# Two attention blocks on one core: the divisors of the linear attention computed behind the softmax sums instead of behind the gather

## The chip, the cores and the metric

The kernel runs on one core of one Trainium2 chip. The metric is the device time of one execution in microseconds. Four runs of the kernel before took 2598.89 to 2601.56 us, with a median of 2601.18.

## The reference, cut to what matters

The input x has 8 images of 512 channels and 64 x 64 = 4096 positions, float32. Two attention blocks follow each other.

```python
# first block: softmax attention over max-pooled keys and values
f = conv1x1(x, Wf, bf)                       # 64 channels
g = maxpool2x2(conv1x1(x, Wg, bg))           # 64 channels, 1024 positions
v = maxpool2x2(conv1x1(x, Wh, bh))           # 256 channels, 1024 positions
s = einsum('bcn,bcm->bnm', f, g)
beta = softmax(s, axis=-1)
o = einsum('bcm,bnm->bcn', v, beta)
x = gamma * conv1x1(o, Wv, bv) + x

# second block: linear attention
Q, K, V = wq @ x + bq, wk @ x + bk, wv @ x + bv
delu = lambda t: 10 * relu(t) + exp(10 * minimum(t, 0))
Qf, Kf = delu(Q).T, delu(K)                  # 64 features
KV = einsum('bmn,bcn->bmc', Kf, V)
norm = 1 / einsum('bnd,bd->bn', Qf, Kf.sum(-1) + EPS)
attn = einsum('bnd,bdc,bn->bcn', Qf, KV, norm)
return x + gamma1 * attn
```

Two divisions matter here. The softmax divides by the sum of exponentials of each position. The second block divides by Qf times the sum of Kf, one divisor for each position; these are the divisors that move.

## The kernel before, in words

**Chunks and steps.** Each image is cut into 8 chunks of 512 positions, 64 chunks in all. The function `step(s)` puts the work of one step in order. In step s the first block is finished for chunk s (its attention, projection and store), the scores of chunk s+1 are computed, and the keys and values of chunk s+9 are prepared. The letter j is the place of chunk s in its image, 0 to 7. The second block lags by one image: while image b goes through the first block, the output of image b-1 is computed in pairs of chunks and added to what is stored. So it is at work in steps 8 to 63 (`c_here`), and the pairs of the last image are done after the loop in another way.

**The order.** The kernel's order is written out by hand. `at(t, fn)` notes a piece of work with a due time t inside the step; the pieces are sorted by t and issued in that order on each engine, which runs its own list in order. A due time is therefore only a place in the list, the same for all five queues: PE (TensorE), DVE (VectorE), ACT (ScalarE), POOL (GpSimd) and SP (SyncE, which issues most DMAs).

**The softmax sums.** The exponentials of chunk s+1 (`weigh`, lines 402 to 411; scores on TensorE at L407, exponentials at L411) are added up on VectorE (L445 to L450). `total` multiplies the result by ones on TensorE. For most chunks (`by_quarters`, chunks 2 to 55) it does so in four matmuls of 128 columns, each into 32 output partitions (L464, shape 128x32), so that the reciprocal (L474) runs on 128 x 128 and not on 128 x 512. `spread_inverses` then writes four rows to DRAM (L479, tile rd) and reads them back onto all partitions (L481, tile rb); `keep_inverses` copies them into PSUM on ScalarE (L485, tile rtot); `look` reads both sums and reciprocals on ScalarE for a check of range (L489, L490). `normalize_block` multiplies the exponentials by rtot in four pieces (L499). For the other chunks the sums are one matmul on all 512 columns (L459) and the reciprocal takes 128 x 512 with no DMA.

**Attention and projection.** `attend` computes the seven products M1 to M7 of one level of a Strassen-like scheme (L523), each of eight 128x256 matmul instructions in the trace, with combinations on VectorE (L532 to L556). `project` does the same with seven products N1 to N7 (L586). Three of them are added into the bank of the first, after each of three evictions by ScalarE (L596), each followed by an addition on GpSimd (L599); VectorE adds the others (L602, L607). The differences of the normalized exponentials for the next chunk follow on VectorE (L505 to L514).

**Around the divisors.** `gather` (L727, tile pg, shape 128x64) multiplies transposed features and transposed x. `features` (L633) and what follows (L643 to L652) make Q and K features; qq holds the Q features of a pair of chunks, 64 partitions each. `normalize(pair, at, t, t_invert, t_out)` has three pieces:

- `product` at t: four matmuls into 32 output partitions each (L818, tile pd), by a matrix kb that holds the sums of K features. The trace shows them as eight instructions, since each float32 matmul is two.
- `inversion` at t_invert: the reciprocal on VectorE (L825, tile rq_pd, which shares its one buffer with L474's rq), a DMA that writes eight rows to DRAM (L827), and two DMAs that read them back onto 64 partitions each (L831, tile rn).
- `out` at t_out: VectorE multiplies qq by rn (L837).

`normalize` is called in steps with j=0 for the first pair of the image, and with j = 1, 3, 5 for the next ones: 4 times for each of 7 images, 28 in all. `finish`, in steps with odd j, multiplies qq by KV (L855), copies to y (L858) and adds y to the output in DRAM with two DMAs of GpSimd's queue (L861).

**Due times near the change.** In the steps concerned: gather 12.6; M6 14.4; sums 16.1 in odd j with `c_here`, else 17.85 (19.55 in the last image's even steps); M5 16.2; M7 17.9; M4 19.6; reciprocal of the sums 18.0, their DMAs 18.01; transposes of v (uv, L371) 18.7; VectorE's last combination of the attention products 22.5; `keep_inverses` 23.0; first normalization 24.3. Those are the values for the middle of the run.

**Buffers.** All PSUM tiles come from one pool of 8 banks, scratch tiles from a pool of 7. A tile takes the buffer that came free earliest in the written order, and its first instruction waits for the last reader of the tile before it.

Of the kernel before, what the change touches and what calls it, by code (L numbers as in the profile page):

```python
# [51 lines left out]
def tile_two_attention_blocks(  # L52
# [32 lines left out]
    TOTAL = B * NCHUNK  # L85
# [91 lines left out]
    def half(e):  # L177
        return slice(e * D, (e + 1) * D)

    def run(ctx, general):  # L180
# [14 lines left out]
        def bank(name):  # L195
            return psum.tile([P, CH], F32, tag="m", name=name)

        def scratch(name):
            return temp.tile([P, CH], F32, tag="t", name=name)
# [610 lines left out]
        def normalize(pair, at, t, t_invert, t_out):  # L810

            m = {}

            def product():

                pd = m["pd"] = bank(f"pd_{pair}")[:, 0:P]
                for i in range(NT):
                    nc.tensor.matmul(  # L818
                        pd[bass.ts(i, QP), :], kb[:, D - QP // 2 : D + QP // 2],
                        qq[pair][:, bass.ts(i, P)], start=True, stop=True,  # L820
                    )

            def inversion():
                rd = work1.tile([P, P], F32, tag="rq", name=f"rq_pd_{pair}")
                nc.vector.reciprocal(rd, m["pd"])  # L825
                d = rows.tile([2 * NT, P], F32, tag="rn", name=f"rn_{pair}_row")
                nc.sync.dma_start(out=d, in_=rd[0 : P : QP // 2, :])  # L827
                rn = m["rn"] = scratch(f"rn_{pair}")
                for e in range(2):
                    row = d.rearrange("(i e) n -> e i n", e=2)[e : e + 1]  # L830
                    nc.sync.dma_start(  # L831
                        out=rn[half(e)].rearrange("p (i n) -> p i n", n=P),
                        in_=row.to_broadcast([D, NT, P]),
                    )

            def out():
                nc.vector.tensor_tensor(qq[pair], qq[pair], m["rn"], ALU.mult)  # L837

            at(t, product)
            at(t_invert, inversion)  # L840
            at(t_out, out)
# [114 lines left out]
        def step(s):  # L956
            here, after = 0 <= s < TOTAL, 0 <= s + 1 < TOTAL
            a = s + LEAD
# [3 lines left out]
            pair = (b_c * NCHUNK + j) // 2  # L962
# [57 lines left out]
            if c_here and here and j == 1 and a <= TOTAL:  # L1020
                make_KV(b_c, at, 5.5, 5.55)
            if c_here and here and j == 0:
                normalize(pair, at, 12.65, 13.7, 38.6)
            if c_here and here and j % 2 == 1 and j < NCHUNK - 1:
                normalize(pair + 1, at, 12.65, 13.7, 38.6)
            if c_here and here and j % 2 == 1:

                cover = a == TOTAL
# [119 lines left out]
        for s in range(-LEAD, TOTAL + 1):  # L1148
            step(s)
# [59 lines left out]
```

## Time and profile before

| | |
|---|---|
| median of 4 runs | 2601.18 us (2598.89 to 2601.56) |
| the profiled execution | 2602.07 us |
| its span | 2600.3 us |
| mean granted TensorE clock | 0.995 |
| busy: TensorE, VectorE, ScalarE, GpSimd | 2564.4, 1954.2, 1587.0, 771.8 us |
| L818 (divisors) on TensorE | 224 instructions, median 285 ns |
| L464 (sums in quarters) on TensorE | 432 instructions, median 285 ns |
| L825, L474 (reciprocals, 128x128) | 28 of 951 ns, 54 of 957 ns (medians) |
| L474 (reciprocals, 128x512) | 10 of 3367 ns |
| L837 (multiplication by rn) | 28 of 682 ns |

The span is that of the profiled execution alone; the difference to its time lies before the first and behind the last instruction. In the timeline a row gives start, length, engine, line, operation and tiles, and the number of instructions merged into it; a bracket at its end tells how long the engine had stood idle before it, and what ended that. TensorE's instructions overlap: a row's length reaches beyond the start of the next, so costs on TensorE are read as differences of starts.

### The profile page before, as it was taken

The numbers are of one execution on the slowest core, as the hardware profiler recorded it, in microseconds if no ns is written. First come the engines' busy times: TensorE is split into PE (matmuls) and PEld (weight loads), VectorE is DVE, ScalarE is ACT, GpSimd is POOL, SyncE is SP. The second block draws the span as 40 slices with busy tenths as digits, with TensorE's granted clock in tenths as the row PEclk, the third lists the DMA queues.
The fourth block names the chain that finished last, engine by engine and source line by source line (L and its number), as shares of the span: only waits on it lengthen the run. The fifth ranks groups of instructions, "written<-read, shape, count | busy, mean of one in ns | idle before, by whom it ended". The sixth has DMA issues, their size and how long they took to land.

```text
span 2600.3 us, 32002 instructions
## 1 busy us (share of the span) xinstructions
PE 2564.4 (99%) x11207; PEld 1766.8 (68%) x11207; DVE 1954.2 (75%) x3000; ACT 1587.0 (61%) x2724; POOL 771.8 (30%) x618
## 2 busy tenths in 40 slices
PE   9999999999999999999999999999999999999997
PEld 6667767667667667677666676666676676766664
DVE  5777777777777777777777777777777777788874
ACT  3365566566565676675675665666755656656662
POOL 5422323322323323223233233323233232221112
PEclk9999999999999999999999999999999999999998
DMA  5154455575555675565665565755657655665658
GB/s 179 46 140 98 128 146 144 132 178 140 148 165 133 165 176 127 157 165 130 173 153 152 148 142 152 188 133 150 159 132 183 148 145 146 146 147 144 162 141 270
DMA packets 488730, 390.68 MB, mean 150 GB/s; under 512 B 342072, under 2 KB 357360, under 8 KB 488560
## 3 DMA queue, kind: packets, MB, share of 16 engines
q1 hardware_dynamic: 471312, 329.03, 45.9%
q0 software_dynamic: 15232, 58.72, 12.1%
q8 instruction: 91, 1.49, 0.2%
q10 hardware_dynamic: 2016, 0.79, 0.1%
q14 instruction: 79, 0.65, 0.1%
HBM read 173.41 MB, written 133.39 MB: 118 GB/s over the span
## 4 chain that ended last, share of the span: by engine, by line
PE 91%; DVE 3%; DMA 1%; issue 1%; ACT 0%; POOL 0%; DVEq 0%; ACTq 0%; SPq 0%
PE M L523 30%; PE N L586 14%; PE H L316 13%; PE s L407 9%; PE pk L633 8%; PE fg L272 7%; PE pg L727 5%; PE pa L855 4%; PE tot L464 1%; DVE E L499 1%; PE pkv L791 1%; PE pa L934 1%; PE pd L818 0%; DMA rb<-rd 0%; PE tot L459 0%
## 5 line engine op out<-in xcount | busy, mean ns | idle before, releaser
L599 POOL TENSOR_TENSOR xb<-xb,n 128x512 f32<-128x512 f32 x192 | 245.6, 1279 | 470.4 <-ACT n L596 459.9
L523 PE MATMUL M<-T,S 128*128 128x256 f32 x1536 | 365.6, 389 | 0.0
L499 DVE TENSOR_TENSOR E<-E,rtot 128x1024 f32<-128x1024 f32 x256 | 307.6, 1223 | 71.1 <-ACT rtot L485 69.0
L523 PEld LDWEIGHTS M<-T,S 128*128 128x128 f32 x1536 | 283.6, 191 | 81.4 <-ACT E L411 24.9
L695 ACT COPY xT<-u 128x1024 uint16<-128x1024 uint16 x252 | 328.3, 1354 | 1.4
L682 ACT COPY w<-xb 128x1024 uint16<-128x1024 uint16 x252 | 244.8, 1042 | 87.7 <-DVE xb L602 87.7
L596 ACT ACTIVATE n<-N,gb_v 128x256 f32<-128x256 f32 x384 | 160.8, 470 | 216.7 <-PE N L586 216.7
L411 ACT ACTIVATE E<-s 128x512 f32<-128x512 f32 x512 | 257.0, 624 | 33.5 <-DVE T L514 18.9
L674 POOL COPY kT<-uk 128x512 uint16<-128x512 uint16 x56 | 67.3, 1202 | 620.7 <-DMA uk<-wk 620.7
L586 PE MATMUL N<-to,w_v 128*128 128x256 f32 x1024 | 243.6, 380 | 4.1 <-ACT n L596 3.9
L407 PE MATMUL s<-f,g 64*128 64x512 f32 x1024 | 240.2, 604 | 2.8 <-DVE o L532 2.8
L523 PE MATMUL M<-E,vT 128*128 128x256 f32 x1024 | 231.8, 379 | 2.1 <-DVE E L499 2.1
L633 PE MATMUL pk<-xb,w_kqk 128*128 128x512 f32 x512 | 230.5, 593 | 1.9 <-DVE xb L607 1.9
L305 POOL TENSOR_TENSOR tha<-xa 128x512 f32<-128x512 f32 x59 | 80.2, 1360 | 500.7 <-PE M L523 463.9
L602 DVE TENSOR_TENSOR xb<-xb,N 128x512 f32<-128x512 f32 x256 | 173.9, 683 | 56.7 <-POOL xb L599 54.4
L586 PEld LDWEIGHTS N<-to,w_v 128*128 128x128 f32 x1024 | 193.2, 190 | 34.0 <-ACT n L596 7.0
L523 PEld LDWEIGHTS M<-E,vT 128*128 128x128 f32 x1024 | 194.4, 190 | 29.7 <-issue 3.4
L272 PE MATMUL fg<-xa,w_fg 128*128 128x512 f32 x472 | 212.5, 593 | 0.0
L445 DVE TENSOR_TENSOR r<-E 128x1024 f32<-128x1024 f32 x64 | 78.4, 1225 | 166.3 <-ACT E L411 166.3
L586 PE MATMUL N<-o,w_v 128*128 128x256 f32 x768 | 188.4, 381 | 1.8 <-ACT n L596 0.9
L586 PEld LDWEIGHTS N<-o,w_v 128*128 128x128 f32 x768 | 144.6, 190 | 56.6 <-issue 35.7
L485 ACT COPY rtot<-rb 128x512 f32<-128x512 f32 x54 | 31.8, 589 | 241.3 <-DMA rb<-rd 241.3
(160 smaller groups left out, 4515.3 us busy)
## 6 DMA issues: line engine op xcount, KB each, us to landing
xb<-in_x_dram SPq DMA_DIRECT2D x64, 1024.0 KB
out_dram<-xb SPq DMA_DIRECT2D x63, 1024.0 KB
xa<-in_x_dram SPq DMA_DIRECT2D x59, 1024.0 KB
out_dram<-y POOLq DMA_DIRECT2D x56, 1024.0 KB, 10.5
rb<-rd SPq DMA_DIRECT2D x54, 256.0 KB
w_v<-in_L_conv_wv_dram SPq DMA_DIRECT2D x8, 1024.0 KB
rn<-rn_row SPq DMA_DIRECT2D x56, 128.0 KB
x_early<-in_x_dram SPq DMA_DIRECT2D x4, 1024.0 KB
```

Of the source, the lines that this page charges most:

```text
L272: nc.tensor.matmul(fg, w_fg[:, k, :], x_a[a][:, k, :], start=(k == 0), stop=(k == KT - 1))
L316: nc.tensor.matmul(m[i], w_h7[i][:, k, :], th[a][i][:, k, :], start=(k == 0), stop=(k == hk - 1))
L407: nc.tensor.matmul(sc[e], g[half(e), i, :], fs[s][half(e), :], start=True, stop=True)
L411: nc.scalar.activation(es[s][:, 2 * i + e, :], sc[e], AF.Exp)
L499: nc.vector.tensor_tensor(b, b, r, ALU.mult)
L523: nc.tensor.matmul(m[i], v7[i][:, k, :], te[s][i][:, k, :], start=(k == 0), stop=(k == hm - 1))
L586: nc.tensor.matmul(a[:, k, :], w_v7[i][:, bass.ts(k, P)], b, start=not more and k == 0, stop=True, skip_group_check=more or k > 0,)
L599: nc.gpsimd.tensor_tensor(of_x(*ij), of_x(*ij), u, ALU.add)
L602: nc.vector.tensor_tensor(of_x(*ij), of_x(*ij), m[i], op)
L633: nc.tensor.matmul(pk, w_kqk[:, i, e * D : (e + 2) * D], x_b[s][:, i, :], start=(i == 0), stop=(i == KT - 1),)
L682: nc.scalar.copy(w, x_b[s][:, k, :].bitcast(U16).rearrange("p (n h) -> p h n", h=2))
L695: nc.scalar.copy(v[:, k], u)
```

## The change

The divisors' matmuls, their reciprocal and the DMAs behind it get later due times. The matmuls go from 12.65, directly behind the gather, to 17.87 (19.57 in the first step of the last image); the reciprocal and the three DMAs from 13.7 to 22.6. The multiplication by the result stays at 38.6. No instruction is added or removed.

```diff
             if c_here and here and j == 0:
-                normalize(pair, at, 12.65, 13.7, 38.6)
+                normalize(pair, at, 17.87 if a < TOTAL else 19.57, 22.6, 38.6)
             if c_here and here and j % 2 == 1 and j < NCHUNK - 1:
-                normalize(pair + 1, at, 12.65, 13.7, 38.6)
+                normalize(pair + 1, at, 17.87, 22.6, 38.6)
```

In the order of the built program this means, for the steps before the last image: on TensorE, from gather, **pd**, M6, M5, tot, M7, M4 to gather, M6, M5, tot, **pd**, M7, M4 where j=0; from gather, **pd**, M6, tot, M5, M7, M4 to gather, M6, tot, M5, **pd**, M7, M4 where j is 1, 3 or 5. On VectorE the reciprocal L825 goes from ahead of L537 to behind L556, directly ahead of the first L499. On SP the row write and the two reads go from ahead of L479 to behind L371. In the last image the sums are the 512-column form (L459), and the block goes from behind the gather to behind L459 (first step) or behind M5 (odd steps).

## The prediction

> **What bounds the kernel now.** I read the page, the waits and then the timeline around the divisors. From the page:
>
> ```profile
> span 2600.3 us, 32002 instructions
> ...
> PE 2564.4 (99%) x11207; PEld 1766.8 (68%) x11207; DVE 1954.2 (75%) x3000; ACT 1587.0 (61%) x2724; POOL 771.8 (30%) x618
> ...
> PE 91%; DVE 3%; DMA 1%; issue 1%; ACT 0%; POOL 0%; DVEq 0%; ACTq 0%; SPq 0%
> ```
>
> TensorE holds 91% of the chain. What an edit is worth is thus read in TensorE's own row, as what it adds to it plus the places where it stands still. The view of waits:
>
> ```profile
> DVE rq L474 <- DMA rn_row<-rq_pd: 19.5, 22, 2.2
> ...
> POOL xb L599 <- DMA rn<-rn_row: 10.4, 1, 10.4
> ```
>
> The first line is the wait that the change takes away: both reciprocals write one buffer (tag rq), so the one of the sums (L474) waits until the divisors' row (L827) has been read out of it, 22 times, 19.5 us. Whether that costs anything is a question to TensorE. Its timeline in step 9 (j=1: divisors), step 10 (none), and in step 55, where the attention products run with neither block between them:
>
> ```profile
> 460.65 0.43 PE L818 MATMUL pd<-qq,kb 128*32 128x128 f32 x8
> 461.00 1.99 PE L523 MATMUL M<-T,S 128*128 128x256 f32 x8
> 462.93 0.42 PE L464 MATMUL tot<-r,ones 128*32 128x128 f32 x8
> 463.28 3.72 PE L523 MATMUL M<-T,S 128*128 128x256 f32 x16
> 466.84 1.89 PE L523 MATMUL M<-T,vT 128*128 128x256 f32 x8
> ...
> 498.30 3.72 PE L523 MATMUL M<-T,S 128*128 128x256 f32 x16
> 501.95 0.42 PE L464 MATMUL tot<-r,ones 128*32 128x128 f32 x8
> 502.30 1.99 PE L523 MATMUL M<-T,S 128*128 128x256 f32 x8
> 504.13 1.89 PE L523 MATMUL M<-T,vT 128*128 128x256 f32 x8
> ...
> 2276.44 5.45 PE L523 MATMUL M<-T,S 128*128 128x256 f32 x24
> 2281.73 1.46 PE L523 MATMUL M<-T,vT 128*128 128x256 f32 x6
> ```
>
> Read starts, not durations. Twenty-four products alone take 2281.73 - 2276.44 = 5.29. With the sums among them, 504.13 - 498.30 = 5.83: a 128x32 block alone between 128x128 products costs 0.55 (0.54 by the rounded starts, 0.553 unrounded). The divisors, which now stand between pg (128x64) and the products, add only 461.00 - 460.65 = 0.35: there the shape of the array changes anyway.
>
> Last, where TensorE stands still. From the start of the score matmuls (L407) of one step to the next, every step with j=1, 3 or 5 of images 1 to 6 takes 41.08, every plain even one 37.29: no waiting that varies. The six j=0 steps take 41.17, 40.78, 40.42, 40.80, 40.55 and 42.32. The first:
>
> ```profile
> 419.61 0.95 DVE L825 RECIPROCAL rq_pd<-pd 128x128 f32<-128x128 f32 x1
> ...
> 422.96 1.32 SPq L831 DMA_DIRECT2D rn<-rn_row  x2
> 423.03 0.96 DVE L474 RECIPROCAL rq<-tot 128x128 f32<-128x128 f32 x1 [2.20 <-DMA rn_row<-rq_pd]
> ...
> 426.56 0.35 SPq L481 DMA_DIRECT2D rb<-rd  x1
> ...
> 429.93 0.59 ACT L485 COPY rtot<-rb 128x512 f32<-128x512 f32 x1 [3.74 <-DMA rb<-rd]
> ...
> 431.33 0.92 PE L586 MATMUL N<-to,w_v 128*128 128x256 f32 x3 [0.30 <-ACT n L596]
> ```
>
> The late reciprocal makes the spread sums (rb) late; ScalarE stands at L485; the eviction n (L596) is queued behind it; TensorE's sixth projection product needs that eviction. In step 48 the same place idles 1.45. Step 24 has no such wait, so the excess over 40.42 is what there is to win: 0.75 + 0.36 + 0 + 0.38 + 0.13 + 1.90 = 3.52 us.
>
> **The change part by part.** All 28 divisor blocks (j = 0, 1, 3, 5 of seven images) move.
>
> *TensorE, j=0 of images 1 to 6.* The block follows the sums directly, in the same 128x32 shape. Not in the trace: two such blocks in a row. Within the sums' block the second round of four starts 0.113 after the first, so two rounds cost 0.23; the other bound is today's 0.356, which would be no change. I take 0.226, the nearest row, being of the same form: 6 x -0.13 = -0.8.
>
> *TensorE, j=1, 3, 5.* Here the sums stand at 16.1 and M5 at 16.2, so the block at 17.87 falls between M5 and M7, alone, not behind the sums. It costs 0.553, the sums' own row, in place of 0.356: +0.197, 21 times: +4.1. Bounds: no more than today (0), and twice the difference (+8.3), for want of a row that shows more.
>
> The Trainium skill (TensorEngine Tiling (Array Packing), Key Properties) says that a change of tiling mode drains the engine. It speaks against this half of the change: in odd steps the block adds two changes of mode in place of one, in j=0 none in place of one. The trace agrees that a change costs, 0.13 beside pg (0.356 - 0.226) and 0.16 each for the lone block (half of 0.553 - 0.226). If every change had one price between these, the odd steps would lose 2.7 to 3.4 and the j=0 steps win 0.8 to 1.0, and the sum below would be 0.5 to 1.0 lower.
>
> *VectorE, quarters.* L474 no longer waits for the row, so rtot comes earlier. In step 8: M6 starts 0.35 earlier, the sums' matmul at 419.70, its reciprocal at about 420.2 (0.5 behind, as at 502.44) instead of 423.03. By that step's own delays rd is issued at 421.2, rb at 423.4, and rtot is copied at 426.7 instead of 429.93. The eviction needs its product at 429.4, so 2.7 us are to spare; step 48, where rb took 5.0 to land instead of 3.4, still has about 1. I take the whole stall as gone: -3.5; bounds 0 and -3.5. In odd steps rtot comes 1.1 earlier and TensorE does not notice.
>
> *VectorE, the moved reciprocal (0.95).* It now stands behind L556 and ahead of the first normalization (L499). In step 8 L556 now ends about 425.9, so the reciprocal is done at 426.9, when rtot has just come; the normalization still starts 3.6 before its 430.55. In step 9 L556 ends at 470.53 + 0.20, the reciprocal at 471.68, where L499 began at 471.82: hidden by what was the wait for rtot. It waits for the look (L490) and for rd, both done by then. Without that cover 0.95 would fall on L499; its last one ends at 478.18 and its first user on VectorE (L505) starts at 482.18, so 4 us remain.
>
> *The last image.* Step 56 has no rd/rb. Its 3.37 us reciprocal starts 0.36 earlier with the sums, but from there VectorE is busy without a gap to L532 at 2340.20, for which the score matmuls stand still. The 0.95 that filled a wait before now lies in that row: 0.95 - 0.36 = +0.6 (bounds -0.4, the stall at L553 alone, and +0.95). In steps 57, 59 and 61 the 0.92 wait ahead of L652 takes it up; their +0.2 on TensorE is in the 21 above.
>
> *SyncE and DMAs.* The row write (4 KB) and its two reads (2 x 128 KB) pass behind rd, rb and the transpose uv, which gain. They now start at 471.7 in odd steps, after this:
>
> ```profile
> 469.53 2.54 POOL L861 DMA_DIRECT2D out_dram<-y  x2
> ```
>
> These two accumulations keep the DMA engines busy until about 482. The last image shows the pair under such a load: row write at 2473.13, reads at 2478.99, landed by 2485.37 (the 10.4 line above): 5.9 and 12.2. From 472.3 that gives the reads at 478.2, landing at 484.5. Behind the reads SyncE has the transposes u, first issued at 482.29: 2.2 to spare after 1.9 of issuing. L837 needs the data at 490.2: 5.7 to spare. In step 56 the next load of x moves from 2322.5 to about 2330, and is used at 2360. No cost; if the cover went, see the third rival.
>
> The Trainium skill (DMA: Bandwidth & Descriptors, Queues, rings and completion order) has each engine take the queues in turn, packet by packet. By that the reads would land soon after their issue, about 480 in place of 484.5; the sum is the same.
>
> *PSUM and scratch.* The pools hand out other buffers from the moved tile on. N1 of odd steps now waits for the look (done 465.97, needed 472.0), pk for an addition done at 479.5 (needed 482.15), pg of step 57 for the divisors' reciprocal, 6 us ahead. No cost.
>
> **Sum** against the profiled execution, 2602.07 (span 2600.3 and 1.8 around it; 0.89 above the median 2601.18): -0.8 + 4.1 - 3.5 + 0.6 = +0.4, that is 2602.5 there, and 2601.6 beside the median.
>
> **Rivals.**
> 1. *The stalls of j=0 stay* (rb lands late for another reason, as the 5.0 in step 48 hints): 2601.6 + 3.5 = 2605.1. Against it: 2.7 us to spare.
> 2. *A lone divisor block costs no more than beside pg.* The 4.1 falls away: 2597.5. For it: bounds only; against it: the sums' row, the same form.
> 3. *The reads of the divisors come too late* (the other side, slower). They start 10 us later, into the accumulations. If they land after 490.2, L837 holds L511, L514 and L532 queued behind it on VectorE; L532 frees the bank for the third pair of score matmuls (loaded at 494.62, L532 ends 493.49, so 1.1 to spare). It decides from 19.0 us between row write and landing (490.2 - 472.3 + 1.1), where 12.2 were seen; at 20 it would cost 1.0 in each of 18 odd steps: 2601.6 + 18 = 2620.
> 4. *The freed wait is worth more than the j=0 stalls* (VectorE 19.5 us earlier in sum). If all of it reached TensorE: 2601.6 + 3.5 - 19.5 = 2585.6. Against it: odd steps of one length to 0.01 us.
>
> **How the numbers follow.** A measurement of this kernel tells about 0.2% (5.2 us) from no change. Forecast 0.58, rival 1 0.10, rival 2 0.08, rival 3 0.16, rival 4 0.08. Rivals 1 and 2 stay within 0.2%, so same 0.76, slower 0.16, faster 0.08. The range leaves out rivals 3 and 4, 0.24 together, of which the mild end of 3 still falls inside: from rival 2, 2597.5, to the doubled price of the lone block, 2601.6 + 4.1 = 2605.7, so 2606.
>
> **What would show it.** Rq's line of waits on rn_row gone; step 8 and its like at 40.3 from score to score; odd steps at 41.28 (41.08 would be rival 2); L837 without a wait for rn; step 56's score matmuls idle 0.6 longer. A line of waits of L837 on rn, or odd steps of unequal length, would make the forecast wrong.

## The result, and the profile after

The changed kernel took 2604.15 us (median of 40 runs, 2603.03 to 2606.98), the kernel before 2601.17 (median of 60 runs beside them, 2597.62 to 2604.25). The ratio is 1.0014, with a 95% interval of 1.0009 to 1.0018: slower by 2.3 to 4.7 us, about 3.0, where 0.4 was forecast. That lies within the 0.2% that the prediction counted as no change, and within its range of 2597.5 to 2606, but it is seven times its sum, so a term of that sum was mis-sized.

The profiled execution of the changed kernel took 2603.87 us (before: 2602.07). From its page:

```profile
span 2602.0 us, 32060 instructions
...
PE 2562.2 (98%) x11207; PEld 1764.3 (68%) x11207; DVE 1959.1 (75%) x3000; ACT 1587.3 (61%) x2724; POOL 775.0 (30%) x618
...
PE 87%; DVE 6%; ACT 1%; issue 1%; DMA 0%; POOL 0%; DVEq 0%; ACTq 0%; SPq 0%
```

TensorE still has the chain, but VectorE has doubled its share of it, from 3 to 6%, and is busy 4.9 us longer with the same 3000 instructions. Some VectorE instruction got longer. The view of waits has what the change promised:

```profile
DVE E L499 <- ACT rtot L485: 29.1, 26, 1.3
...
DVE rq L474 <- PE tot L464: 20.1, 25, 0.9
...
PEld N L586 <- ACT n L596: 7.0, 9, 1.3
```

(engine, tile and line, who ended the wait: total us, times, longest). L474's line on the divisors' row is gone; the normalizations' wait for rtot fell from 69.0 us to 29.1, and the wait of the projection's weight loads (PEld) for the eviction from 10.4 to 7.0. The products themselves had waited for it in steps 8 and 48 (0.30 and 1.45 us); in images 1 to 6 they no longer do.

Where the time went is read step by step, as the difference of starts of the first score matmul (L407) of one step and the next, in the timelines of the two profiled executions:

| steps | before | after | forecast |
|---|---|---|---|
| 8, 16, 24 (j=0) | 41.17, 40.78, 40.42 | 40.79, 40.80, 40.79 | 40.3 each |
| 32, 40, 48 (j=0) | 40.80, 40.55, 42.32 | 40.28, 40.80, 40.78 | 40.3 each |
| 18 odd ones (j=1, 3, 5) | 41.08 each | 41.28 each | 41.28 each |
| 18 even ones (j=2, 4, 6) | 37.29 each | 37.29, step 42: 37.73 | 37.29 each |
| 56 and 57 together | 66.37 | 66.98 | +0.6, +0.2 |
| 59, 61 | 32.55, 32.55 | 32.74, 32.74 | +0.2 each |

The odd steps came out to a hundredth. The six j=0 steps did not: 246.04 became 244.25, a gain of 1.8 where 4.3 was forecast. Only step 32 has the forecast length; the five others stop at 40.8. The timeline of the changed kernel in step 8 shows why:

```profile
417.30 1.39 POOL L305 TENSOR_TENSOR tha<-xa 128x512 f32<-128x512 f32 x1 [7.36 <-PE M L523]
417.60 1.64 DVE L450 TENSOR_TENSOR r<-r 128x512 f32<-128x512 f32 x1
...
419.39 0.43 PE L464 MATMUL tot<-r,ones 128*32 128x128 f32 x8 [0.44 <-DVE r L450]
...
419.61 0.43 PE L818 MATMUL pd<-qq,kb 128*32 128x128 f32 x8
...
420.10 0.94 DVE L474 RECIPROCAL rq<-tot 128x128 f32<-128x128 f32 x1
...
426.10 0.59 ACT L485 COPY rtot<-rb 128x512 f32<-128x512 f32 x1 [0.35 <-DMA rb<-rd]
...
428.91 0.84 ACT L596 ACTIVATE n<-N,gb_v 128x256 f32<-128x256 f32 x2 [2.22 <-PE N L586]
...
429.57 2.75 PE L586 MATMUL N<-to,w_v 128*128 128x256 f32 x12
```

and the timeline of the kernel before, at the same place. (Step 8 starts at 409.72 in the changed kernel and at 410.54 before; so 0.82 is to be added to the changed kernel's times to compare.)

```profile
418.40 0.69 DVE L450 TENSOR_TENSOR r<-r 128x512 f32<-128x512 f32 x1
418.47 1.75 POOL L305 TENSOR_TENSOR tha<-xa 128x512 f32<-128x512 f32 x1 [7.74 <-PE M L523]
```

From 420.10 down, the changed kernel does what was forecast: the reciprocal follows the sums, rtot is copied 16.4 us into the step (before: 19.4), the eviction waits for its product and no longer the other way round, and the projection products run without a gap. But the sums' matmul now waits 0.44 for L450, the last addition of the exponentials on VectorE. L450 takes 1.64 us instead of 0.69. Beside it runs GpSimd's L305, a difference of two parts of x, which starts when M6 ends. Before, M6 was held up by the divisor block; L305 began 7.93 into the step, 0.07 behind L450, and was itself stretched to 1.75 (its length where it is alone: 1.27). Now M6 ends 0.35 earlier, L305 begins at 7.58, and that is 0.30 ahead of L450. In both kernels it is the later of the two that is stretched. Step 32 escapes because L450 starts there 7.47 into the step, before and after, some 0.4 earlier than in the five others; it is 0.32 ahead of L305 and keeps its 0.69 us.

The Trainium skill (SBUF — State Buffer, Who interferes with whom) describes this: VectorE and GpSimd share a pair of ports as an exclusive lock, and of two instructions that need it, the one that issues second is blocked. The rows above agree: 0.69 against 1.64 us, and 1.27 against 1.75 the other way round.

The groups of instructions by form count the effect over the whole run. The changed kernel (columns: line, engine, operation, count | busy us, mean ns | idle us before it and what ended most of it):

```profile
L450 DVE TENSOR_TENSOR r<-r 128x512 f32<-128x512 f32 x64 | 52.0, 812 | 2.2
...
L464 PE MATMUL tot<-r,ones 128*32 128x128 f32 x432 | 23.0, 284 | 2.6 <-DVE r L450 2.6
```

The kernel before:

```profile
L450 DVE TENSOR_TENSOR r<-r 128x512 f32<-128x512 f32 x64 | 45.3, 707 | 2.2
```

L450 grew by 6.7 us, that is by seven long ones. One of them is in step 0, ahead of all that was moved (the kernel before with only GpSimd's work moved, below, has it too). From step 8 on it takes 1.64 us or more six times after and never before, and exactly six times, for 2.6 us in all, TensorE waits for it: in five j=0 steps, and by the same collision in step 42, the one even step that got longer.

The two profiles also differ at the two ends of the run, by the clock. TensorE's busy time and PEclk in two stretches, before:

```profile
107.30:149.50 42.20, 39.93 (x149) 27.91 (x148) 35.25 (x52) 21.80 (x38) 9.62 (x8) 0.92 0.21 40
2563.00:2566.40 3.40, 3.40 (x18) 1.74 (x15) 0.36 (x1) 1.14 (x2) 0.00 (x0) 0.50 0.12 41
```

and after:

```profile
107.30:149.50 42.20, 38.34 (x152) 26.36 (x152) 37.81 (x52) 22.75 (x38) 11.88 (x8) 1.00 0.23 47
2563.00:2566.40 3.40, 3.40 (x33) 2.95 (x34) 0.30 (x2) 1.41 (x3) 0.00 (x0) 1.00 0.73 267
```

The granted clock is the third figure from the end: 0.92 and 0.50 before, 1.00 and 1.00 after. These stretches (1.1 us in step 0, 0.7 behind the last step) made this one execution of the kernel before longer, and have nothing to do with the change: step 0 holds no divisor block, and took 42.25 and 42.24 us at 0.92 in the profiles of two of the experiments below, 40.6 to 41.1 at 0.96 or 1.00 in all others. That is why the two profiled times differ by 1.8 and the medians by 3.0. Without them, the steps sum to: 18 x 0.198 = +3.6 in the odd steps, +0.4 in 59 and 61, +0.6 in 56 and 57, -1.8 in the j=0 steps, +0.4 in step 42: +3.2.

### The profile page after: what moved, and what is told of

Its sections match the earlier page's. It is cut to its first block, busy times and chain, and to the rows that moved or that the text cites. A ratio compares the mean times of both kernels' runs of the same rounds, so it can differ in the third digit from the quotient of the medians.

```text
span 2602.0 us, 32060 instructions
## 1 busy us (share of the span) xinstructions
PE 2562.2 (98%) x11207; PEld 1764.3 (68%) x11207; DVE 1959.1 (75%) x3000; ACT 1587.3 (61%) x2724; POOL 775.0 (30%) x618
## 4 chain that ended last, share of the span: by engine, by line
PE 87%; DVE 6%; ACT 1%; issue 1%; DMA 0%; POOL 0%; DVEq 0%; ACTq 0%; SPq 0%
PE M L523 28%; PE N L586 14%; PE H L316 12%; PE s L407 8%; PE pk L633 8%; PE fg L272 7%; PE pg L727 4%; PE pa L855 4%; PE tot L464 1%; DVE E L499 1%; DVE r L447 1%; ACT E L411 1%; PE pa L934 1%; PE pkv L791 1%; DVE r L450 0%
## 5 line engine op out<-in xcount | busy, mean ns | idle before, releaser
L695 ACT COPY xT<-u 128x1024 uint16<-128x1024 uint16 x252 | 328.1, 1353 | 1.8 <-DMA u<-w 0.4
L499 DVE TENSOR_TENSOR E<-E,rtot 128x1024 f32<-128x1024 f32 x256 | 306.2, 1218 | 30.6 <-ACT rtot L485 29.1
L407 PE MATMUL s<-f,g 64*128 64x512 f32 x1024 | 239.6, 603 | 3.3 <-DVE o L532 3.3
L305 POOL TENSOR_TENSOR tha<-xa 128x512 f32<-128x512 f32 x59 | 79.6, 1349 | 488.1 <-PE M L523 448.4
L407 PEld LDWEIGHTS s<-f,g 64*128 64x128 f32 x1024 | 95.5, 186 | 116.0 <-issue 94.5
```

The lines of the kernel that those rows point to most:

```text
L407: nc.tensor.matmul(sc[e], g[half(e), i, :], fs[s][half(e), :], start=True, stop=True)
L499: nc.vector.tensor_tensor(b, b, r, ALU.mult)
L695: nc.scalar.copy(v[:, k], u)
```

## The experiments

The theory: a lone divisor block costs 0.2 in odd steps; behind the sums it saves 0.13; the j=0 stalls go; and 0.5 of that gain is lost in five j=0 steps because GpSimd's L305 gets ahead of VectorE's L450. The rivals: the 0.5 comes from the divisors' block or the reciprocal themselves, not from GpSimd; the odd steps' loss is in the late reads and not in the shape of the block. Each diff is against the changed kernel unless it says otherwise, and each time is beside the kernel before of the same set of runs.

### Only the j=0 steps are moved

```diff
-                normalize(pair + 1, at, 17.87, 22.6, 38.6)
+                normalize(pair + 1, at, 12.65, 13.7, 38.6)
```

> Only the seven j=0 blocks are moved as in the change; those of j=1, 3, 5 stay at 12.65 and 13.7. My theory adds up the change step by step: the six j=0 steps of images 1 to 6 as the changed kernel's trace shows them (together 1.8 us shorter than before, most of them at 40.79), the last image's first two steps +0.4. Sum -1.4, so about 2599.8 beside 2601.2, with every odd step back at 41.08. Rival: the cost comes from the later DMAs or from the later reciprocal, wherever the matmuls stand; then the j=0 steps carry part of the 3 us and this kernel is slower than before, by up to 1 us.

Measured: 2599.77 us against 2600.25, ratio 0.9996 (0.9987 to 1.0005). The odd steps are back at 41.08, and the six j=0 steps are as in the changed kernel, five at 40.8 and step 32 at 40.28. So the 0.5 of the j=0 steps does not come from the odd steps' later reads. Steps 56 and 57 take 0.42 more than before; with their own lone block taken off, the changed kernel has the same (0.61 - 0.20). The forecast had 0.6 here.

### Only the odd steps are moved

```diff
-                normalize(pair, at, 17.87 if a < TOTAL else 19.57, 22.6, 38.6)
+                normalize(pair, at, 12.65, 13.7, 38.6)
```

> Only the 21 blocks of j=1, 3, 5 are moved. Theory: each costs 0.197 us more as a block alone between two 128x128 products, so +4.1 and about 2605.3; the odd steps at 41.28, the j=0 steps as before (40.4 to 42.3, with the wait of the sums' reciprocal on the divisors' row still there in them). Rival: the late DMAs cost something beside; then the odd steps are longer than 41.28, or L837 waits for its DMA.

Measured: 2607.69 us against 2600.25, ratio 1.0027 (1.0017 to 1.0037): 7.4 more, where 4.1 were expected. The odd steps take 41.28 as forecast, with j=0 left alone. As far as the steps show the excess, it lies in the j=0 steps, 248.1 against 246.0, and in step 59 (0.4 longer, where 0.2 was expected). The wait that the change removes is still there in the j=0 steps. This kernel's view of waits:

```profile
DVE rq L474 <- PE tot L464: 20.7, 25, 0.9
...
DVE rq L474 <- DMA rn_row<-rq_pd: 11.7, 6, 2.3
```

Six times, once for each j=0 step of images 1 to 6, L474 waits for the row; it starts 12.2 to 13.1 us into the step there, where before it starts 11.8 to 12.5. TensorE's projection products wait for the eviction in five of these steps, 0.25 to 0.65 each. Why the untouched j=0 steps got longer when the odd ones were moved was not settled; only in step 32 does the collision of L450 with L305 show (L450 1.80 long).

### The matmuls stay, only the reciprocal and its DMAs go later

```diff
-                normalize(pair, at, 17.87 if a < TOTAL else 19.57, 22.6, 38.6)
+                normalize(pair, at, 12.65, 22.6, 38.6)
...
-                normalize(pair + 1, at, 17.87, 22.6, 38.6)
+                normalize(pair + 1, at, 12.65, 22.6, 38.6)
```

> All 28 divisors' matmuls stay at 12.65 behind the gather; only the reciprocal and its three DMAs go to 22.6. Theory: nothing changes on TensorE, the stall of the j=0 steps goes (-3.5), and the sums' matmul is not reached early, so that VectorE's last sum (L450) keeps its 0.69 us; in step 56 the reciprocal costs its whole 0.95. Sum -2.6, about 2598.6, j=0 steps at 40.42. Rival: that the gain needs the matmuls' move; then the j=0 steps stay above 40.42 and the time near 2601.2.

Measured: 2598.62 us against 2600.25, ratio 0.9993 (0.9984 to 1.0002). Odd steps 41.08, all six j=0 steps 40.42: the whole 3.5 of stalls is won, by moving one reciprocal and three DMAs and no matmul. Steps 56 and 57 take 0.8 more than before, for the 0.95 expected. Its timeline in step 8, which starts at 410.65:

```profile
420.65 0.96 DVE L474 RECIPROCAL rq<-tot 128x128 f32<-128x128 f32 x1 [0.52 <-PE tot L464]
...
426.78 0.59 ACT L485 COPY rtot<-rb 128x512 f32<-128x512 f32 x1 [0.49 <-DMA rb<-rd]
...
429.46 0.84 ACT L596 ACTIVATE n<-N,gb_v 128x256 f32<-128x256 f32 x2 [2.08 <-PE N L586]
```

With the matmuls in their old place, M6 ends as late as before, L450 keeps its 0.69 us in step 8, and TensorE does not wait for it. So the reciprocal is not what stretches L450, and the odd steps' 0.2 belongs to the matmuls alone: this kernel issues the row write and the reads where the changed one does.

### GpSimd's differences in another order in j=0 steps

Of its four differences GpSimd computes the third first. That one writes a tile that M7 has read (tag T3), not one that M6 has read (tag T2), so GpSimd starts later. This adds three lines, so later lines are numbered three higher.

```diff
+                if a > LEAD and a % NCHUNK == LEAD % NCHUNK:
+                    nc.gpsimd.tensor_tensor(t3, b22, b12, ALU.subtract)
                 nc.gpsimd.tensor_tensor(t1, b12, b11, ALU.subtract)
                 nc.gpsimd.tensor_tensor(t2, b22, t1, ALU.subtract)
-                nc.gpsimd.tensor_tensor(t3, b22, b12, ALU.subtract)
+                if not (a > LEAD and a % NCHUNK == LEAD % NCHUNK):
+                    nc.gpsimd.tensor_tensor(t3, b22, b12, ALU.subtract)
```

> The changed kernel, and in the j=0 steps of images 1 to 6 GpSimd's four differences of x are reordered, so that the first of them waits for M7 and not for M6, and runs behind VectorE's last sum instead of into it. Theory: VectorE's L450 takes 1.64 us in those steps because GpSimd's L305 runs beside it; apart from each other it takes 0.69, the sums' matmul does not wait, and the j=0 steps go from 40.79 to 40.29: -2.5, about 2601.7. Rival: L450 is late by itself, since VectorE's sums are late in these steps; then it still ends about 9.5 us behind the first score matmul and the steps stay at 40.79, 2604.2.

Measured: 2601.27 us against 2600.25, ratio 1.0004 (0.9995 to 1.0013). All six j=0 steps now take 40.28. Its timeline in step 8, which starts at 409.66 (L453, L467 and L821 are what were L450, L464 and L818):

```profile
417.53 0.69 DVE L453 TENSOR_TENSOR r<-r 128x512 f32<-128x512 f32 x1
...
418.82 0.43 PE L467 MATMUL tot<-r,ones 128*32 128x128 f32 x8
419.06 0.40 PE L821 MATMUL pd<-qq,kb 128*32 128x128 f32 x8
...
421.47 1.27 POOL L306 TENSOR_TENSOR thb<-xa 128x512 f32<-128x512 f32 x1 [11.60 <-DVE to L547]
```

VectorE, TensorE and the divisor block are those of the changed kernel; only GpSimd moved. The last addition is 0.69 long again and the sums' matmul starts 9.16 into the step without a wait, where it starts at 9.67 in the changed kernel. (The bracket at L306 names VectorE's L547, which ended at that same moment; by the code it is M7 that this instruction has to wait for.) This settles the missing 2.5 us: it was GpSimd, not the block and not the reciprocal.

### The same edit of GpSimd in the kernel before

The diff above, put into the kernel before, with the divisors in their old place.

> The kernel before, with nothing but the reorder of GpSimd's differences in the j=0 steps of images 1 to 6. Theory: there the divisors' block keeps TensorE from the sums' matmul until VectorE is done, so L450 (0.69 us) was not what TensorE waited for, and the stall behind the late reciprocal of the sums stays: j=0 steps between 40.42 and 42.3, time within 1 us of before. Rival: running GpSimd's work later helps the j=0 steps by itself; then they fall below 40.42.

Measured: 2601.48 us against 2601.28, ratio 1.0000 (0.9990 to 1.0010); the j=0 steps sum to 246.19 (before: 246.04). Where GpSimd does not get ahead of L450, there is nothing to win by moving it. So what the edit brought above was a price of the change.

### The divisors directly behind the sums in odd steps too

```diff
-                normalize(pair + 1, at, 17.87, 22.6, 38.6)
+                normalize(pair + 1, at, 16.11 if a < TOTAL else 17.87, 22.6, 38.6)
```

> The changed kernel with the blocks of j=1, 3, 5 of images 1 to 6 at 16.11, really behind the sums (16.1) and ahead of M5. Theory: the second 128x32 block adds its two rounds alone, 0.226, so that an odd step takes 41.28 - 0.33 = 40.95, 0.13 less than before; 18 of them make -5.9 against the changed kernel, about 2598.3. Rival: a block costs 0.356 wherever it stands beside another narrow one; then the odd steps take 41.08 and the time is 2600.6.

Measured: 2599.37 us against 2601.11, ratio 0.9991 (0.9982 to 1.0000). The odd steps take 40.94, that is 0.34 less than in the changed kernel and 0.14 less than before. The time is 1.1 above the expected 2598.3: without the edit of GpSimd all six j=0 steps, step 32 too, take 40.8 here, and step 42 37.73. The timeline of TensorE in step 9:

```profile
460.53 1.99 PE L523 MATMUL M<-T,S 128*128 128x256 f32 x8
462.46 0.43 PE L464 MATMUL tot<-r,ones 128*32 128x128 f32 x8
462.70 0.40 PE L818 MATMUL pd<-qq,kb 128*32 128x128 f32 x8
463.03 3.72 PE L523 MATMUL M<-T,S 128*128 128x256 f32 x16
```

against the changed kernel's, where the same block stands between two products:

```profile
459.45 1.99 PE L523 MATMUL M<-T,S 128*128 128x256 f32 x8
461.38 0.42 PE L464 MATMUL tot<-r,ones 128*32 128x128 f32 x8
461.73 1.99 PE L523 MATMUL M<-T,S 128*128 128x256 f32 x8
463.66 0.43 PE L818 MATMUL pd<-qq,kb 128*32 128x128 f32 x8
464.01 1.99 PE L523 MATMUL M<-T,S 128*128 128x256 f32 x8
```

Read by starts, the two blocks together take 463.03 - 462.46 = 0.57 and the sums alone 461.73 - 461.38 = 0.35, so the second block adds 0.22. The steps with j=7, odd ones without a divisor block, give the price for all three places: they take 40.73 in images 1 to 5, in these two kernels and in the one before. Against them the same four matmuls cost 0.21 behind a block of their own shape (40.94), 0.35 beside the gather (41.08) and 0.55 alone between products (41.28). Rival 2, that a lone block costs no more than beside the gather, is refuted by the one row, and its remedy stands in the other. The reads are issued about as late as in the changed kernel (26.6 into step 9, there 27.6), so the odd steps' loss came from the block's place between products of another shape.

### All that helped, together

In images 1 to 6 both kinds of step take the block directly behind the sums, with the order of GpSimd's differences as above; the last image keeps the old places.

```diff
-                normalize(pair, at, 17.87 if a < TOTAL else 19.57, 22.6, 38.6)
+                normalize(pair, at, *((17.87, 22.6) if a < TOTAL else (12.65, 13.7)), 38.6)
...
-                normalize(pair + 1, at, 17.87, 22.6, 38.6)
+                normalize(pair + 1, at, *((16.11, 22.6) if a < TOTAL else (12.65, 13.7)), 38.6)
```

> Images 1 to 6: j=0 as in the change with GpSimd's differences reordered; j=1, 3, 5 behind the sums at 16.11, reciprocal at 22.6. Last image as before. Theory: -3.5 for the stalls, 24 blocks at 0.13 less (-3.1), nothing lost: about 2594.6, j=0 steps at 40.29, odd steps at 40.95. Rival: with both shortened, VectorE or GpSimd becomes late in the j=0 or odd steps; then one of these step lengths is not reached, and the time lies between 2594.6 and 2601.

Measured: 2593.49 us (2593.22 to 2594.41) against 2601.11, ratio 0.9970 (0.9957 to 0.9982): faster than both kernels, by 7.6 us against the one before. All j=0 steps take 40.28 and all odd ones of images 1 to 6 40.94, which makes 246.04 - 241.69 = 4.35 and 18 x 0.14 = 2.5 less, together 6.8; the 0.8 beyond that is well inside the interval of the ratio (4.7 to 11.2 us). Its page:

```profile
span 2591.7 us, 32056 instructions
...
PE 2556.4 (99%) x11207; PEld 1769.0 (68%) x11207; DVE 1969.3 (76%) x3000; ACT 1586.6 (61%) x2724; POOL 770.7 (30%) x618
```

VectorE is busier here than in any kernel above, and the kernel is the fastest: its busy time alone says nothing of the kernel's.

### How much room the reads have

In odd steps of images 1 to 6 the reciprocal and its DMAs are put off further, some 7 us further into the accumulations. This asks for the point at which rival 3 becomes true.

```diff
-                normalize(pair + 1, at, 17.87, 22.6, 38.6)
+                normalize(pair + 1, at, 17.87, 29.25 if a < TOTAL else 22.6, 38.6)
```

> The changed kernel, with the reciprocal and the three DMAs of j=1, 3, 5 in images 1 to 6 put off further, from 22.6 to 29.25, behind the last normalization. It asks how much room the third rival of the prediction had. Theory: the reciprocal ends some 8 us later, the row write starts where the accumulations end, SyncE waits for it some 2 to 5 us and the transposes u start up to 4 us later than before; L837 then waits up to 3 us for its reads. If ScalarE's L695 and VectorE's L837 take this up, the odd steps stay at 41.28; if not, they grow by up to 3 us each, 54 in all. Rival: the DMAs have room to spare even so, and nothing changes.

Measured: 2615.46 us against 2601.28, ratio 1.0058 (1.0041 to 1.0075). First the changed kernel's timeline of SyncE in step 9, and then this kernel's, in the order of time and with other engines:

```profile
470.44 0.60 SPq L827 DMA_DIRECT2D rn_row<-rq_pd  x1
478.10 1.35 SPq L831 DMA_DIRECT2D rn<-rn_row  x2
481.30 5.36 SPq L688 DMA_TRANSPOSE u<-w  x4
```

```profile
477.45 0.60 SPq L827 DMA_DIRECT2D rn_row<-rq_pd  x1
482.21 1.90 SPq L831 DMA_DIRECT2D rn<-rn_row  x2
484.22 5.43 SPq L688 DMA_TRANSPOSE u<-w  x4
487.58 1.35 ACT L695 COPY xT<-u 128x1024 uint16<-128x1024 uint16 x1 [1.07 <-DMA u<-w]
...
494.41 3.95 ACT L411 ACTIVATE E<-s 128x512 f32<-128x512 f32 x8
...
500.10 1.37 POOL L305 TENSOR_TENSOR tha<-xa 128x512 f32<-128x512 f32 x1 [6.58 <-PE M L523]
500.39 1.64 DVE L450 TENSOR_TENSOR r<-r 128x512 f32<-128x512 f32 x1
...
502.18 0.43 PE L464 MATMUL tot<-r,ones 128*32 128x128 f32 x8 [0.48 <-DVE r L450]
```

Step 9 starts at 450.52 in the changed kernel and at 450.76 in this one, step 10 at 491.80 and 492.04. The row write comes 6.8 later into the step, and now it does cost, but by another road than the one that rival 3 named. L837 has no wait for rn in this kernel either. It is the transposes u, queued on SyncE behind the reads, that start 33.5 into the step and not 30.8. ScalarE waits for them at L695, so its exponentials begin 2.4 into step 10 (1.2 in the changed kernel, at 493.00), L450 follows at 8.35 (7.17), and L305, at 8.06, is ahead of it. This kernel's view of waits:

```profile
ACT xT L695 <- DMA u<-w: 12.1, 19, 1.8
...
PE tot L464 <- DVE r L450: 8.5, 19, 0.5
```

Of the 18 steps that follow a moved odd step, 13 take 37.73 to 39.02 instead of 37.29. In each of these 0.37 to 0.51 is TensorE's wait for L450; the six j=0 steps, which have it in this kernel as well, make up the 19 waits of the view. In the longer ones the last score matmuls come late too, and the gather (L727) behind them starts 0.43 later in step 10 than in the changed kernel, and 1.18 later in step 22, the longest; that these matmuls wait for the late exponentials is the likely reason, but only in step 22 does the trace name it.

## Why the prediction was right or wrong

**Odd steps, +0.197 each: right.** 0.198 was measured in all 18 of images 1 to 6, about 0.2 in 57, 59 and 61. The estimate from the sums' own row, the same form of block between the same products, held. The aside on one price for every change of mode was added up wrongly: the change has 21 - 6 = 15 more of them, at 0.13 to 0.16 that is 2.0 to 2.5 in place of 3.3, so the sum would have been 0.9 to 1.4 lower, not 0.5 to 1.0. The measured +0.198 here and -0.14 in the next line are not one price.

**j=0, block behind the sums, -0.13 each: right.** Step 32 and all six steps of the kernel with GpSimd moved take 40.28, 0.14 less than the 40.42 of the kernel in which only the reciprocal was moved.

**The stalls of j=0, -3.5: the mechanism right, the sum with the line above mis-sized.** The wait on rn_row and the stall at the projection went as forecast; rtot was copied 16.4 into step 8, where 16.2 was worked out (426.7 in the trace of before). But of -4.3 in all only -1.8 arrived. The step that failed is in "VectorE, quarters": "M6 starts 0.35 earlier, the sums' matmul at 419.70". That is 9.16 into step 8; it started at 9.67, with a wait of 0.44, and alike in five steps of six. The prediction moved TensorE's row forward and left VectorE's last addition L450 where it stood. Of its own it would have been in time: it ended 8.55 into the step before, and 8.56 in the kernel with GpSimd moved, 0.6 ahead of the sums' matmul at 9.16. What was not asked is what M6's earlier end releases: GpSimd's L305, which then held up that very addition, so that it ended at 9.52. The row that told of it was in the trace of before, L305 at 418.47 with 1.75 us, 0.07 behind L450: a pair that an edit of 0.35 makes change places.

**Step 42, +0.44: not foreseen.** The same collision in an even step, in one of eighteen, but here it is VectorE that comes late. Step 42 starts at 1760.24; L305 begins 7.63 into it as before, L450 at 7.71 and not at 7.18. The changed kernel's timeline at the end of step 41 and in step 42, in the order of time:

```profile
1749.74 6.53 SPq L688 DMA_TRANSPOSE u<-w  x4
1755.15 1.34 ACT L695 COPY xT<-u 128x1024 uint16<-128x1024 uint16 x1 [0.44 <-DMA u<-w]
...
1767.87 1.26 POOL L305 TENSOR_TENSOR tha<-xa 128x512 f32<-128x512 f32 x1 [6.64 <-PE M L523]
1767.95 1.74 DVE L450 TENSOR_TENSOR r<-r 128x512 f32<-128x512 f32 x1
```

ScalarE waited for the transposes u, the road that the last experiment shows. They began on time, 30.8 into step 41, with the reads issued at 26.8, but took 6.53 us to issue instead of 5.36 as in step 9. What made that issue longer, and whether the moved DMAs had a part in it, is not shown.

**The moved reciprocal: right.** In step 8 it starts at 425.78 and ends at 426.74, with the copy of rtot (426.69) for which L499 would have waited. VectorE stood 0.24 us ahead of it for the look (L490), which had been taken to be done by then.

**The last image: right in kind, a little too dear.** +0.6 was forecast for step 56 and 0.2 for the block in 57; the two steps together took 0.61 more, so the reciprocal cost 0.41. The place is the one that was named, score matmuls behind L532, in the first microseconds of step 57: the last four instructions start 4.23 behind the first scores (2342.47 - 2338.24), where it was 3.40 before (2340.66 - 2337.26). (The description of the change above puts the block of the last image's odd steps behind the gather before the change; it stood behind the output products pa, shape 64x128, another shape just the same, with the same 0.356 to the next start, and the gather comes later there.)

**SyncE and DMAs, no cost: right but perhaps for step 42, with less room than thought.** The row write was issued 19.9 into step 9, as worked out (471.7 in the trace of before, 20.0), but the reads followed 7.66 behind its start, where 0.6 + 5.9 had been added: 27.6 into the step for 26.5. That used up 1.1 of the 2.2 to spare. In all 18 odd steps they followed 6.8 to 7.8 behind. The transposes u start 30.8 into the step, 30.6 before, which is the 0.2 of the block. L837 shows no wait. The semaphore updates in the trace tell when a DMA has landed: the reads' last one comes 32.8 into step 9, which is the 484.5 that was worked out, and 32.0 to 33.2 into the 18 odd steps, at least 5.5 ahead of L837 at 38.7. That the figure came out so well is in part luck, since the row was slower and the reads faster than thought; and in the last image before, whose row was the source, the reads landed by 2487.28 and not by 2485.37, where GpSimd's wait ended. The Trainium skill's rule that each engine takes the queues in turn (DMA: Bandwidth & Descriptors, Queues, rings and completion order) had been read as letting the reads land at about 480, that is 28.3 into the step; the 32.8 does not bear that out.

**The rivals.** 1 (stalls stay) and 2 (lone block free) are refuted by 40.42 in all j=0 steps of the third experiment and by 41.28 in the odd ones. 4 (all of the freed wait counts) is refuted by the odd steps of one length. 3 did not happen; the last experiment shows that a regular cost was less than 7 us away, and that it begins at the transposes and not at L837.

## What to carry to other kernels

Work taken off an in-order engine moves up what stands behind it, and with it the moments at which other engines are set free: before the gain is booked, look at how early the operands of what moves up are ready, and at what the earlier end of its neighbours lets begin on other engines, and beside what. Small matmuls of another array shape are priced by their neighbours: put them behind a block of their own shape, or leave them where the shape changes anyway. When an instruction has two lengths in one trace, look at what runs beside it each time; the order of such a pair may be worth more than the edit.

## What the runs showed of the hardware that had not been expected

- The addition of two tiles on VectorE at L450 (128x512, float32) takes 0.69 us alone, and 1.64 to 1.80 us where GpSimd's subtraction of the same size (L305) began 0.01 to 0.33 us ahead of it. L305 takes 1.27 alone; where it is the second, up to 0.14 us behind, it takes 1.69 to 1.83 and L450 keeps its 0.69. From step 7 on the ten profiled executions hold no exception.
- A 4 KB write and its read-back on SyncE's queue need 7.7 us to the issue of the reads when they start 2 us behind the two accumulating DMAs of GpSimd's queue (step 9 of the changed kernel: row write at 470.44, accumulations issued at 468.53; 6.8 to 7.8 in the 18 odd steps), and 4.8 us when they start 7 us later. In the kernel before, where the pair stands 10.6 into the odd steps and ahead of the accumulations, it is 1.7 to 1.8 us.
- In the profiled execution of the kernel before, TensorE's granted clock was 0.50 in a stretch of 3.4 us near its end and 0.92 in one of 42 us near its start, which went with 1.8 us more in that execution than in the changed kernel's, though its mean clock was 0.995.
